# Small inputs in one transfer, six weight buffers for two sections, and the impulse response's matmuls placed behind named weight rows

## The chip, the cores and the metric

The kernel runs on one core of a Trainium2 chip. A core has a matrix engine (TensorE, PE in the profile; PEld is its weight load), three engines for elementwise work (VectorE or DVE, ScalarE or ACT, GpSimd or POOL) and a sync engine (SP) that issues most of the transfers. Every engine works through its own instruction list in order; engines wait for one another and for transfers through semaphores. The metric is the device time of one execution in microseconds (us). It was 2180.94 us in the median of three runs (2180.49 to 2183.13).

## The reference

One layer with two residual branches over x, of 4 batches x 1024 rows x 2048 columns, float32:

```
mod = silu(c) @ wmod                  # c: 4 x 2048, wmod: 2048 x (6*2048)
sa, ca, ga, sb, cb, gb = six sections of mod; ga, gb: sign kept, size at least 0.25
h = layernorm(x) * (1 + ca) + sa
x = x + ga * (causal convolution of each row of h with K, + D * h)
h = layernorm(x) * (1 + cb) + sb
x = x + gb * (h @ (W + low-rank updates).T + bias)
```

K, 2048 values, is the impulse response of a state space model with 64 complex states. It is computed from Lambda, p, q, Ct (64 complex numbers each), Vc (64 x 64 complex), Bp and log_step: a Cauchy sum at 2048 frequencies, a rational combination of four such sums, and an inverse Fourier transform.

## The kernel before

**Stages.** The kernel has a head, a first phase and a second phase. The first phase goes through 32 blocks of 128 rows: layer norm, modulation, transposition, the convolution as matmuls with a Toeplitz operand of K, gate and residual, second layer norm; the other four sections of `mod` and the merging of W with its low-rank updates are interleaved with it. The second phase multiplies 16 units of 256 rows with the merged weights (Winograd's form, seven products) in two halves.

**The head: two sections of mod.** A section is 16 *weight rows*. One weight row is a tile `wm` of 128 x 2048 float32 (1 MiB, loaded by `mod_load`, L309) and four matmuls by 128 columns x 512 (`mod_mm`, L314) that add into one PSUM tile `modps`. In this text r0 to r15 are the rows of section 1 (it gives `ca`), r16 to r31 those of section 0 (it gives `sa`), and r32 onward those of section 2. The pool of the `wm` tiles has three buffers (`WM = 3`), so the load of row n + 3 waits on SP until the four matmuls of row n are done. All rows and all blocks of x are issued on SP's queue, in order. After a section `mod_column` copies `modps` (ACT, `mrow`), transposes it (PE, `mtp`) and writes the column tile (DVE). `fold_scale` then finds a scale from `ca` and `sa` (a maximum over all partitions on POOL) and multiplies both. The first modulated activation (L535, `t<-tp,sa,ca`) needs that; it is where the convolution's operands begin.

**The head: the impulse response.** `toeplitz` calls `s4`. Sixteen transfers are issued on POOL's queue (L88 to L107): the vectors in two copies, `Vc` in two copies, `Bp`, `log_step`, and four tables. DVE computes scalars and numerators from them (L112 to L155). PE makes cosines and sines at 512 frequencies from the bfloat16 table `t_cs` (L161, `s4cs`), DVE and ACT make 1/w and the numerator from them (L165 to L173, a reciprocal among them), and PE sums over the states (L176, `s4rp`); this is done four times. Then come some forty small DVE instructions (L181 to L226), the transform (L229, `s4kp`), the scaling of K (L242 to L249, with a maximum on POOL), a store of K to DRAM (L254, `kd<-kk`), and a load of 128 shifted copies (L258, `kb<-kd`, 1 MiB). The last two are issued on ACT's queue. Four matmuls with a reversed identity follow (L262, `kbps`), and DVE makes the six fp16 operands `kh` and `kl` (L278 to L283).

**The order.** Most of it is a scheduler's, from the order in which the Python code emits work and from priorities. All of `toeplitz` up to the load of `kb` is emitted in one piece under `tc.high_priority()`, before any section. The part from L260 is emitted behind the matmuls of r22 (`KT = 6` in section 0) with `tc.issue_after`, which keeps later work from being placed ahead of that instruction. Blocks 0, 1 and 2 of x are loaded after r15.

**Completion lanes.** Transfers issued by SP and ACT share eight completion semaphores, handed out in turn. A transfer that gets a semaphore whose last transfer has not landed waits for that landing first, on the queue that issues it. In the kernel before, r23 waits in this way for the store `kd<-kk`, and r25 for the load `kb<-kd`.

The conditions of the head's loop and the constants that the change touches:

```
    for sec in (1, 0):
        for i, _ in enumerate(section(sec)):
            take(mer, M0)
            if sec == 0 and i == KT:
                with tc.issue_after(k.last.ins):
                    take(toe, 1)
        if sec == 1:
            for r in range(3):
                xs[r] = k.conv_load(pl, r)
```

Of the kernel before, what the change touches and what calls it, by code (L numbers as in the profile page):

```python
# [25 lines left out]
D = 2048          # length of a row: model width and sequence of the convolution  # L26
NB = 4            # batches
NC = D // P       # chunks of 128 in a row
HC = NC // 2
NU = 16           # units of 256 rows  # L30
LNMAX = 46.0      # no entry of a layer norm over 2048 exceeds sqrt(2047)
FP_TOP = 4096.0   # fp16 operands are scaled to at most twice this


class Net:
# [11 lines left out]
    # ---- scales: powers of two that bring the largest entry into [top, 2*top)  # L47
# [27 lines left out]
    # ---- impulse response of the state space model: PSUM [l1, l2], l = 16*l1 + l2  # L75
    def s4(self, pool):
# [7 lines left out]
        vec = T([P, 4, 2], "s4vec")  # L84
        vc = T([P, 64, 2], "s4vc")
        for h in range(2):
            hp = slice(64 * h, 64 * h + 64)
            nc.gpsimd.dma_start(out=vec[hp, 0, :], in_=io["Lambda_ri"])  # L88
            nc.gpsimd.dma_start(out=vec[hp, 1, :], in_=io["p_ri"])
            nc.gpsimd.dma_start(out=vec[hp, 2, :], in_=io["q_ri"])  # L90
            nc.gpsimd.dma_start(out=vec[hp, 3, :], in_=io["Ct_ri"].rearrange("o n c -> (o n) c"))
            nc.gpsimd.dma_start(out=vc[hp], in_=io["Vc_ri"])
        bp = T([P, 64], "s4bp")
        nc.gpsimd.dma_start(out=bp, in_=io["Bp"].rearrange("m o -> (m o)").partition_broadcast(P))
        ls = T([P, 1], "s4ls")
        nc.gpsimd.dma_start(out=ls, in_=io["log_step"].partition_broadcast(P))
        # cosines and sines in three bfloat16 parts, summed and broadcast by the tensor engine
        cs = T([3, 2, D], "s4cs", BF16)
        nc.gpsimd.dma_start(out=cs, in_=io["t_cs"])
        one = T([3, P], "s4one", BF16)  # L100
        v.memset(one, 1.0)
        csk = T([P, 2, 16], "s4csk")
        nc.gpsimd.dma_start(out=csk, in_=io["t_csk"])
        tw = T([P, 2, 16, 16], "s4tw")
        nc.gpsimd.dma_start(out=tw, in_=io["t_tw"])
        dft = T([P, 2, P], "s4dft")
        nc.gpsimd.dma_start(out=dft, in_=io["t_dft"])  # L107

        # 2/step = 2*exp(-log_step): range reduction, polynomial, exponent bits
# [16 lines left out]
        # B = Vc Bp  # L126
# [5 lines left out]
        # numerators conj(ct)B, conj(ct)p, conj(q)B, conj(q)p  # L132
# [15 lines left out]
        # 1/w, w = i (2/step) S - lambda C: real part in the first 64 rows, imaginary part below  # L148
# [8 lines left out]
        w = 512  # L157
        for c0 in range(0, D, w):
            cc, sc = (self.acc.tile([P, w], F32, tag="a", name="s4cs") for _ in range(2))
            for i, ps in enumerate((cc, sc)):  # L160
                nc.tensor.matmul(ps, one, cs[:, i, ds(c0, w)], start=True, stop=True)  # L161
# [11 lines left out]
            tt(nu, nu, wr, MUL)  # L173
            for c in range(w // P):
                g = c0 // P + c
                nc.tensor.matmul(  # L176
                    rp[:, g, :], nu[:, ds(P * c, P)], coef,
                    start=(g == 0), stop=(g == NC - 1), skip_group_check=True,
                )
# [36 lines left out]
        # inverse transform: over k2 with the table, over k1 on the tensor engine  # L216
# [5 lines left out]
        for o, (x, y, op) in enumerate(((ar, ai, SUB), (ai, ar, ADD))):  # L222
# [3 lines left out]
            v.tensor_reduce(zz[:, o, :], w1, AX.X, ADD)  # L226
        kp = self.tps.tile([P, 16], F32, tag="t", name="s4kp")
        for c in range(2):
            nc.tensor.matmul(kp, dft[:, c, :], zz[:, c, :], start=(c == 0), stop=(c == 1))  # L229
        return kp  # L230

    # ---- Toeplitz operand kb[s, j] = K[j - s], in two fp16 parts; D is added to K[0]
    def toeplitz(self, pool):
# [7 lines left out]
        kp = self.s4(pool)  # L241
        v.tensor_copy(kk, kp)  # L242
# [12 lines left out]
        # row s starts P - 1 - s earlier; the tensor engine puts the rows in the opposite order  # L255
# [8 lines left out]
        # for outputs in pairs of chunks: K at even chunks (for sums of two operands), and the  # L264
        # differences to the chunk before and after; two fp16 parts each
# [36 lines left out]
    # ---- one section of the modulation: PSUM rows 32 q + b hold columns 512 q ..  # L302
# [18 lines left out]
    def mod_column(self, pool, name, plus_one):  # L321
        """[d in chunk, chunk, batch] of the section in modps"""
# [12 lines left out]
    def mod_gate(self, pool, name, bias=None):  # L335
        """the gate by rows, in DRAM; with bias also gate*bias"""
# [23 lines left out]
    # ---- scales of the normalized, modulated rows, per batch; folded into the columns in place  # L360
# [15 lines left out]
    # ---- low-rank factors in two fp16 parts; w_e and the inverse scale of A go into B  # L376
    def prep_lora(self, pool, tmp):
# [9 lines left out]
        # no entry exceeds the norm of its row  # L387
# [32 lines left out]
    # ---- merged weights of d chunks c and c + 8; the seven right operands in DRAM  # L420
    def merge(self, pool, tmp, c):
# [22 lines left out]
        # no entry exceeds the norm of its row  # L444
# [44 lines left out]
    # ---- phase 1: layer norm, modulation, transposed operand of the convolution  # L489
# [29 lines left out]
    def conv_prep(self, pl, r, x, st, out):  # L519
# [4 lines left out]
        # fp16 parts of the chunks, and of the sums of an even chunk and the odd one after it  # L524
# [70 lines left out]
    def conv_late(self, x, y, sums):  # L595
        """gate and residual of a block whose convolution ran before the gate was there"""
# [6 lines left out]
    # ---- the second layer norm, transposed  # L603
# [21 lines left out]
    def gate_tile(self, pool, b):  # L625
        """the gate of a batch with the scales of the convolution's operands taken off, in all rows"""
# [14 lines left out]
    # ---- phase 2: left operands of the seven products of a unit  # L641
# [48 lines left out]
    def ffn_unit(self, pl, u, q, lf, wc):  # L690
# [34 lines left out]
        # Winograd's form; P4 comes with the opposite sign  # L725
# [28 lines left out]
M0, MR = 0, 2  # L754
# [3 lines left out]
WM = 3  # L758
LEFT0 = 30
KT = 6  # L760
# [11 lines left out]
def net(ctx: ExitStack, tc: tile.TileContext, io):  # L772
# [19 lines left out]
    def section(sec):  # L792
# [37 lines left out]
    toe = k.toeplitz(pool(st, "st", 1))  # L830
    with tc.high_priority():
        take(toe, 1)

    xs, hs = {}, {}
    sts = {}
    for sec in (1, 0):
        for i, _ in enumerate(section(sec)):
            take(mer, M0)
            if sec == 0 and i == KT:
                with tc.issue_after(k.last.ins):  # L840
                    take(toe, 1)
        if sec == 1:
            for r in range(3):
                xs[r] = k.conv_load(pl, r)
            for r in range(2):
                sts[r] = k.stats(pl, xs[r], "1")
    st.close()
    for name, bufs in (("h", 2), ("n", 2), ("t", 2), ("y", 2), ("g", 1), ("nt", 2)):
        pl[name] = pool(left, "p1" + name, bufs)
    def rest():  # L850
        mods = (x for sec in (4, 3, 5) for x in section(sec))
# [18 lines left out]
    def load_w(q, i):  # L870
        """the two halves of a right operand; two of them take the places of x"""
# [29 lines left out]
    sec = section(2)  # L901
# [80 lines left out]
def tables():  # L982
    """cosines and sines; they depend on the shapes alone"""
# [9 lines left out]
    csk = np.stack([np.cos(np.pi * kk / n), np.sin(np.pi * kk / n)], 1).astype(np.float32)  # L993
    ph = 2 * np.pi * (kk[:, None, :] * np.arange(16)[None, :, None] % n) / n
    tw = np.stack([np.cos(ph), np.sin(ph)], 1).astype(np.float32)
    a = 2 * np.pi * ((k1 * np.arange(P)[None]) % P) / P
    dft = (np.stack([np.cos(a), -np.sin(a)], 1) / n).astype(np.float32)
    return dict(t_cs=np.stack(parts), t_csk=csk, t_tw=tw, t_dft=dft)


def layout(inputs):
    g = {n.removeprefix("L0_attn_").removeprefix("L0_ffn_").removeprefix("L0_"): np.asarray(a) for n, a in inputs.items()}
    r = {n: g[n] for n in ("Lambda_ri", "p_ri", "q_ri", "Vc_ri", "Ct_ri", "Bp", "D", "log_step", "bias", "A", "coeffs", "scales", "c", "wmod")}
# [23 lines left out]
```

## Time and profile before

| | us |
|---|---|
| time, median of three runs (lowest to highest) | 2180.94 (2180.49 to 2183.13) |
| span of the profiled execution, first to last instruction | 2174.4 |
| median of the runs less that span | 6.5 |
| PE busy in the span | 2090.6 |
| first weight row's matmuls start | 6.51 |
| r31's matmuls start | 119.34 |
| first modulated activation starts | 125.73 |
| first matmul of the convolution starts | 128.88 |

The profiled execution's own device time is not listed beside its span; the median of the three runs stands in for it. A row of the table of waits reads: engine and line that waited, what it waited for, us in total, number of times, the longest. A row of the table by windows reads: the window, its length, busy us (and instructions) of PE, PEld, DVE, ACT and POOL, the granted PE clock as a share of full speed, the busy share of the 16 DMA engines, and GB/s. A timeline row reads: start, duration, engine, line, operation, tiles, shape, count, and in brackets the idle time before it and what ended it.

### The profile page before, as it was taken

How to read it: one execution, taken by the hardware profiler on the slowest of the kernel's cores; microseconds unless marked ns; L12 is line 12 of the kernel's file. 1: busy time of each engine (PE TensorE's matmuls, PEld its weight loads, DVE VectorE, ACT ScalarE, POOL GpSimd, SP SyncE). 2: the span in 40 equal slices, each digit the busy share in tenths (PEclk: the TensorE clock that was granted, in tenths of full speed). 3: DMA queues.
4: the chain of work that ended last, by engine and by line, in shares of the span. 5: the costliest groups of instructions: out<-in, count | busy, mean ns of one | idle time of the engine just before them, and what ended most of it. 6: DMA issues, size and time to landing. Idle time of an engine off the chain costs nothing.

```text
span 2174.4 us, 28541 instructions
## 1 busy us (share of the span) xinstructions
PE 2090.6 (96%) x11084; PEld 1020.7 (47%) x11084; DVE 1356.8 (62%) x2293; ACT 938.0 (43%) x1795; POOL 11.7 (1%) x28
## 2 busy tenths in 40 slices
PE   4699999999999999999999999999999999999998
PEld 1234555555555555565444444444444444444443
DVE  5637898888989999974666666666533333333333
ACT  0046877767867778863353545454300000000000
POOL 1000000000000000000000000000000000000000
PEclk6589999999999999999999999999999999999999
DMA  7988687888788656747766666666785544544541
GB/s 273 368 325 307 232 315 271 300 313 299 278 307 300 219 204 232 257 136 294 264 223 232 222 219 221 232 223 225 285 332 192 174 164 164 175 165 165 172 157 68
DMA packets 207307, 516.62 MB, mean 238 GB/s; under 512 B 16112, under 2 KB 81665, under 8 KB 180289
## 3 DMA queue, kind: packets, MB, share of 16 engines
q1 hardware_dynamic: 206208, 513.11, 66.3%
q8 instruction: 87, 1.43, 0.3%
q10 hardware_dynamic: 388, 1.16, 0.1%
q0 software_dynamic: 576, 0.54, 0.1%
q14 instruction: 48, 0.39, 0.1%
HBM read 325.89 MB, written 188.85 MB: 237 GB/s over the span
## 4 chain that ended last, share of the span: by engine, by line
PE 64%; DVE 13%; ACT 8%; DMA 6%; issue 2%; SPq 1%; DVEq 0%; ACTq 0%
PE fZ L701 18%; PE fY L701 12%; PE fX L701 11%; PE ya L564 9%; PE yb L564 5%; PE lps L440 3%; PE modps L314 3%; DMA gt<-n2d 2%; DVE lf L662 2%; ACT gt L651 2%; PE tp L620 2%; DVE s L668 1%; ACT t L535 1%; ACT n L611 1%; PE tp L532 1%
## 5 line engine op out<-in xcount | busy, mean ns | idle before, releaser
L701 PEld LDWEIGHTS <-lf 128*128 128x128 f16 x5376 | 526.4, 98 | 642.0 <-issue 10.2
L701 PE MATMUL fZ<-w,lf 128*128 128x512 f16 x2304 | 514.8, 380 | 6.2 <-ACT p L709 6.1
L701 PE MATMUL fX<-w,lf 128*128 128x512 f16 x1536 | 342.6, 379 | 0.0
L701 PE MATMUL fY<-w,lf 128*128 128x512 f16 x1536 | 342.5, 379 | 0.0
L564 PEld LDWEIGHTS <-hc 128*128 128x128 f16 x2304 | 215.7, 98 | 187.9 <-issue 31.9
L717 DVE TENSOR_TENSOR xo<-xo,gb 128x1024 f32<-128x1024 f32 x64 | 78.3, 1224 | 204.6 <-DMA xo<-x1d 204.5
L535 ACT ACTIVATE t<-tp,sa,ca 128x128 f32<-128x128 f32 x512 | 200.1, 471 | 6.0 <-DVE sa L373 3.8
L651 ACT ACTIVATE gt<-gt,sb,cb 128x256 f32<-128x256 f32 x256 | 132.1, 594 | 148.2 <-DMA gt<-n2d 147.4
L564 PE MATMUL ya<-kh,hs 128*128 128x512 f16 (+3 forms) x768 | 192.9, 326 | 0.9 <-ACT hs L543 0.9
L564 PE MATMUL ya<-kh,hc 128*128 128x512 f16 (+3 forms) x768 | 192.7, 326 | 0.5 <-ACT qs L577 0.5
L564 PE MATMUL yb<-kh,hc 128*128 128x512 f16 (+3 forms) x768 | 192.5, 326 | 0.0
L314 PE MATMUL modps<-wm,sct 128*32 128x512 f32 x768 | 132.1, 728 | 27.9 <-DMA wm<-in_wmod 27.9
L564 PEld LDWEIGHTS <-hs 128*128 128x128 f16 x1152 | 107.5, 98 | 96.9 <-issue 15.9
L709 ACT COPY p<-fZ 128x512 f32<-128x512 f32 x64 | 37.3, 583 | 256.9 <-PE fZ L701 256.9
L709 ACT COPY p<-fX 128x512 f32<-128x512 f32 x32 | 18.5, 578 | 268.7 <-PE fX L701 255.7
L564 PE MATMUL ya<-kl,hc 128*128 128x512 f16 (+3 forms) x384 | 125.1, 326 | 0.0
L564 PE MATMUL ya<-kl,hs 128*128 128x512 f16 (+3 forms) x384 | 125.1, 326 | 0.0
L564 PE MATMUL yb<-kl,hc 128*128 128x512 f16 (+3 forms) x384 | 125.1, 326 | 0.0
L661 ACT CAST lf<-s 128x1024 f16<-128x1024 f32 x64 | 67.2, 1050 | 102.5 <-DVE s L668 75.8
L621 ACT COPY nt<-tp 128x512 f32<-128x512 f32 x128 | 74.8, 597 | 60.0 <-PE tp L620 40.9
L544 DVE TENSOR_TENSOR hc<-t,hc 128x512 f16<-128x512 f32 x128 | 87.3, 682 | 6.3 <-ACT hc L543 5.8
L723 DVE TENSOR_TENSOR xo<-xo,fin 128x512 f32<-128x512 f32 x128 | 88.2, 689 | 3.1
(247 smaller groups left out, 2234.3 us busy)
## 6 DMA issues: line engine op xcount, KB each, us to landing
wm<-in_wmod SPq DMA_DIRECT2D x96, 1024.0 KB
lfd<-lf SPq DMA_DIRECT2D x112, 512.0 KB
lf<-lfd SPq DMA_DIRECT2D x112, 512.0 KB
x<-in_x SPq DMA_DIRECT2D x32, 1024.0 KB
x1d<-y SPq DMA_DIRECT2D x32, 1024.0 KB
n2d<-nt SPq DMA_DIRECT2D x128, 256.0 KB
gt<-n2d SPq DMA_DIRECT2D x128, 256.0 KB
xo<-x1d SPq DMA_DIRECT2D x64, 512.0 KB
```

Of the source, the lines that this page charges most:

```text
L314: self.last = self.nc.tensor.matmul(self.modps[32 * g : 32 * g + 32, :], self.sct[:, j].rearrange("p r b -> p (r b)"), w[:, ds(512 * g, 512)],
L440: nc.tensor.matmul(ps, la[:, x, k, h], y[:, k, osl], start=(n == 0), stop=(n == 5))
L535: nc.scalar.activation(t[:, k], tp[:, k], AF.Identity, bias=self.sa[:, c, b : b + 1], scale=self.ca[:, c, b : b + 1],)
L544: v.tensor_tensor(lo[:, sl], src, hi[:, sl], SUB)
L564: nc.tensor.matmul(pf[:, o:512], h, self.kf[f][z][:, ds(k0, 512 - o)], start=first, stop=(i == last and (x, z) == (1, 0)), skip_group_chec ...
L621: nc.scalar.copy(nt, tp)
L651: nc.scalar.activation(t[:, c], t[:, c], AF.Identity, bias=self.sb[:, c, b : b + 1], scale=self.cb[:, c, b : b + 1],)
L661: nc.scalar.copy(hl[:, :, 0, :], s)
L701: nc.tensor.matmul(ps[name], lf[i][:, k, x, :], wc[i][k // 4][:, k % 4, y, :], start=(first and n == 0), stop=(n == 3 * HC - 1), skip_grou ...
L709: nc.scalar.copy(t, ps[name])
L717: v.tensor_tensor(x, x, self.gbias, ADD)
L723: v.tensor_tensor(xs[r][:, h], xs[r][:, h], t, ADD)
```

## The change

There are three edits.

1. The small inputs and `c` are packed on the host's side of the layout into one array `small` of 128 x 265 float32, which SP loads first. The tables `csk`, `tw`, `dft` become one array `t_tab` of 128 x 800. `t_cs`, D and `t_tab` are loaded on ACT's queue. POOL issues no transfers any more.
2. Sections 1 and 0 take their weight rows in turn from two pools of three buffers (`wms` and `wm`), six in all. `wms` lies in the memory of the impulse response's own tiles, which is freed after section 0.
3. `s4` is a generator with stopping points. Its first part is emitted early as before. The parts that hold PE work are emitted behind weight rows counted by n over both sections (17 steps each): `KT = (0, 5, 8, 11, 14, 18, 27)`. The first two `s4cs` tables stand behind r0, the four `s4rp` sums behind r5 (in fact behind the first matmul of r6), r8, r11 and r14, the third and fourth table behind the second and third sum, the transform behind r17, and `kbps` behind r26. Blocks 0, 1, 2 of x are loaded after r20, r26 and r31; the statistics of blocks 0 and 1 follow their loads.

In the changed program's instruction lists DVE's 40 small instructions of `s4` come ahead of the three that make `sct` (the matmuls' left operand, which every weight row needs). The lanes fall differently: r3 waits for `t_cs`, r25 for the store `kd<-kk`, and the load of block 1 of x, with r27 to r31 behind it on SP, for the load `kb<-kd`. From some 1750 matmul instructions (of 19900 on PE) and some 120 transfers (of 900 on SP) onward, the lists of every engine are the same as before.

```
+        sm = self.small
+        vec = sm[:, 0:8].rearrange("p (i c) -> p i c", c=2)
+        vc = sm[:, 8:136].rearrange("p (n c) -> p n c", c=2)
+        bp, ls = sm[:, 136:200], sm[:, 200:201]
+
         cs = T([3, 2, D], "s4cs", BF16)
-        nc.gpsimd.dma_start(out=cs, in_=io["t_cs"])
+        nc.scalar.dma_start(out=cs, in_=io["t_cs"])
...
+        tab = T([P, 800], "s4tab")
+        nc.scalar.dma_start(out=tab, in_=io["t_tab"])
...
+        def table(c0):
+            cps[c0] = [self.acc.tile([P, w], F32, tag="a", name="s4cs") for _ in range(2)]
+            for i, ps in enumerate(cps[c0]):
+                nc.tensor.matmul(ps, one, cs[:, i, ds(c0, w)], start=True, stop=True)
+
+        yield
+        table(0)
+        table(w)
         for c0 in range(0, D, w):
-            cc, sc = (self.acc.tile([P, w], F32, tag="a", name="s4cs") for _ in range(2))
-            for i, ps in enumerate((cc, sc)):
-                nc.tensor.matmul(ps, one, cs[:, i, ds(c0, w)], start=True, stop=True)
+            if c0 >= 2 * w:
+                table(c0)
+            cc, sc = cps[c0]
...
             tt(nu, nu, wr, MUL)
+            yield
             for c in range(w // P):
...
+        yield
         kp = self.tps.tile([P, 16], F32, tag="t", name="s4kp")
...
-        c = pool.tile([P, NB, 16], F32, tag="mc", name="mc")
-        nc.sync.dma_start(out=c, in_=self.io["c"].rearrange("b (p j) -> p b j", j=16))
+        self.small = pool.tile([P, 265], F32, tag="small", name="small")
+        nc.sync.dma_start(out=self.small, in_=self.io["small"])
+        c = self.small[:, 201:265].rearrange("p (b j) -> p b j", j=16)
...
-WM = 3
+WM, WMS = 3, 3
+X0 = (21, 27)
 LEFT0 = 30
-KT = 6
+KT = (0, 5, 8, 11, 14, 18, 27)
...
-            k.mod_mm(k.mod_load(wmp, sec, q), q)
+            k.mod_mm(k.mod_load(pools[q % len(pools)], sec, q), q)
...
+    wms = pool(st, "wms", WMS)
     with tc.high_priority():
         take(toe, 1)
...
+    n = 0
     for sec in (1, 0):
-        for i, _ in enumerate(section(sec)):
-            take(mer, M0)
-            if sec == 0 and i == KT:
-                with tc.issue_after(k.last.ins):
+        for _ in section(sec, (wms, wmp)):
+            if n in KT:
+                with tc.issue_after(k.last.ins), tc.high_priority():
                     take(toe, 1)
-        if sec == 1:
-            for r in range(3):
+            if n in X0:
+                r = X0.index(n)
                 xs[r] = k.conv_load(pl, r)
-            for r in range(2):
                 sts[r] = k.stats(pl, xs[r], "1")
+            n += 1
+    xs[2] = k.conv_load(pl, 2)
     st.close()
```

More of the change, by code (lines that the diff above doesn't have):

```diff
@@ L82, in T @@
             return pool.tile(shape, dt, tag=name, name=name)
[L84 to L96, printed above, removed]
+        sm = self.small
+        vec = sm[:, 0:8].rearrange("p (i c) -> p i c", c=2)
+        vc = sm[:, 8:136].rearrange("p (n c) -> p n c", c=2)
+        bp, ls = sm[:, 136:200], sm[:, 200:201]
         cs = T([3, 2, D], "s4cs", BF16)
-        nc.gpsimd.dma_start(out=cs, in_=io["t_cs"])
+        nc.scalar.dma_start(out=cs, in_=io["t_cs"])
         one = T([3, P], "s4one", BF16)
         v.memset(one, 1.0)
[L102 to L107, printed above, removed]
+        tab = T([P, 800], "s4tab")
+        nc.scalar.dma_start(out=tab, in_=io["t_tab"])
+        csk = tab[:, 0:32].rearrange("p (c k) -> p c k", c=2)
+        tw = tab[:, 32:544].rearrange("p (c k n) -> p c k n", c=2, k=16)
+        dft = tab[:, 544:800].rearrange("p (c k) -> p c k", c=2)
         z = T([P, 4], "s4z")
@@ L157, in s4 @@
         w = 512
+        cps = {}
+        def table(c0):
[5 more added lines that the diff above has]
+        table(w)
         for c0 in range(0, D, w):
-            cc, sc = (self.acc.tile([P, w], F32, tag="a", name="s4cs") for _ in range(2))
-            for i, ps in enumerate((cc, sc)):
-                nc.tensor.matmul(ps, one, cs[:, i, ds(c0, w)], start=True, stop=True)
+            if c0 >= 2 * w:
+                table(c0)
+            cc, sc = cps[c0]
             wi = pool.tile([P, w], F32, tag="s4wi", name="s4wi", bufs=2)
@@ L229, in s4 @@
             nc.tensor.matmul(kp, dft[:, c, :], zz[:, c, :], start=(c == 0), stop=(c == 1))
-        return kp
+        self.kp = kp
     def toeplitz(self, pool):
@@ L240, in toeplitz @@
         kk = pool.tile([P, 16], F32, tag="kk", name="kk")
-        kp = self.s4(pool)
-        v.tensor_copy(kk, kp)
+        yield from self.s4(pool)
+        v.tensor_copy(kk, self.kp)
         dt = pool.tile([1, 1], F32, tag="dt", name="dt")
@@ L752 @@
 ACTNORM = ""
-M0, MR = 0, 2
+MR = 2
 ACC, TPS = 5, 2
@@ L790, in net, with section @@
     k.prep_mod(msm)
-    def section(sec):
+    def section(sec, pools):
         for q in range(16):
@@ L850, in rest @@
     def rest():
-        mods = (x for sec in (4, 3, 5) for x in section(sec))
+        mods = (x for sec in (4, 3, 5) for x in section(sec, (wmp,)))
         n = 0
@@ L899, in stats @@
         sts[r] = k.stats(pl, xs[r], "1")
-    sec = section(2)
+    sec = section(2, (wmp,))
     take(prep(0), 9)
@@ L992, in tables @@
     kk = k1 + P * np.arange(16)[None]
-    csk = np.stack([np.cos(np.pi * kk / n), np.sin(np.pi * kk / n)], 1).astype(np.float32)
+    csk = np.stack([np.cos(np.pi * kk / n), np.sin(np.pi * kk / n)], 1)
     ph = 2 * np.pi * (kk[:, None, :] * np.arange(16)[None, :, None] % n) / n
-    tw = np.stack([np.cos(ph), np.sin(ph)], 1).astype(np.float32)
+    tw = np.stack([np.cos(ph), np.sin(ph)], 1)
     a = 2 * np.pi * ((k1 * np.arange(P)[None]) % P) / P
-    dft = (np.stack([np.cos(a), -np.sin(a)], 1) / n).astype(np.float32)
-    return dict(t_cs=np.stack(parts), t_csk=csk, t_tw=tw, t_dft=dft)
+    dft = np.stack([np.cos(a), -np.sin(a)], 1) / n
+    tab = np.concatenate([t.reshape(P, -1) for t in (csk, tw, dft)], 1).astype(np.float32)
+    return dict(t_cs=np.stack(parts), t_tab=tab)
 def layout(inputs):
     g = {n.removeprefix("L0_attn_").removeprefix("L0_ffn_").removeprefix("L0_"): np.asarray(a) for n, a in inputs.items()}
-    r = {n: g[n] for n in ("Lambda_ri", "p_ri", "q_ri", "Vc_ri", "Ct_ri", "Bp", "D", "log_step", "bias", "A", "coeffs", "scales", "c", "wmod")}
+    r = {n: g[n] for n in ("D", "bias", "A", "coeffs", "scales", "wmod")}
+    half = [g[n].reshape(64, -1) for n in ("Lambda_ri", "p_ri", "q_ri", "Ct_ri", "Vc_ri")]
+    both = np.tile(np.concatenate(half, 1), (2, 1))
+    rows = [np.broadcast_to(g[n].reshape(1, -1), (P, g[n].size)) for n in ("Bp", "log_step")]
+    r["small"] = np.concatenate([both, *rows, g["c"].reshape(NB, P, 16).transpose(1, 0, 2).reshape(P, -1)], 1)
     r["x"] = g["u"].reshape(-1, D)
```

## The prediction

> **What bounds the kernel now.** I read PE's waits before and after 130 us first, then SP's waits in the head, then the head cut into windows, then the timeline where the head ends.
>
> PE's waits, and SP's, from 0 to 130 us:
>
> ```profile
> PE modps L314 <- DMA wm<-in_wmod: 27.9, 18, 6.5
> PE s4cs L161 <- DMA s4cs<-in_t_cs: 9.4, 1, 9.4
> PE s4rp L176 <- DVE s4nu L173: 6.0, 4, 2.2
> ...
> SPq L309 <- PE modps L314: 81.4, 32, 14.9
> SPq L309 <- DMA wm<-in_wmod: 23.5, 13, 5.7
> SPq L309 <- DMA kb<-kd: 5.7, 1, 5.7
> ```
>
> PE waits for weight rows, and SP, which loads them, waits for PE to free a buffer. PE works in order, so a matmul of the impulse response that stands in line (9.4 us for `t_cs`) also holds up the weight rows behind it, and with three buffers the loads then stop. The windows show it:
>
> ```profile
> 30.00:34.00 4.00, 2.38 (x6) 0.59 (x4) 3.72 (x16) 0.00 (x0) 0.00 (x0) 0.50 0.03 9
> ...
> 77.00:82.00 5.00, 3.88 (x20) 0.40 (x16) 3.99 (x17) 0.20 (x1) 0.00 (x0) 0.51 1.01 415
> ...
> 93.00:100.00 7.00, 6.88 (x12) 2.68 (x16) 1.19 (x3) 1.17 (x2) 0.00 (x0) 0.58 0.61 243
> ...
> 129.00:160.00 31.00, 30.97 (x193) 12.18 (x191) 12.72 (x25) 16.38 (x43) 0.00 (x0) 1.00 0.86 309
> 160.00:200.00 40.00, 40.00 (x249) 19.90 (x246) 26.24 (x50) 19.47 (x40) 0.00 (x0) 1.00 0.85 310
> ```
>
> Where nothing stops it the DMA runs at a share of 1.01 and 415 GB/s, or 2.5 us for each 1 MiB row (r17 to r20 start at 75.16, 77.65, 80.15 and 82.68). From 30 to 34 us it stands still, and from 93 to 105 it is two thirds busy. From 129 us PE is full. So the program is a head bound by transfers with holes, then a long stretch bound by PE: over 129 to 700 us PE is busy 562 of 571 us. What the head saves, the end should save.
>
> The tail of the head, on the timeline:
>
> ```profile
> 70.88 0.17 DVE L242 COPY kk<-s4kp 128x16 f32<-128x16 f32 x1 [0.53 <-PE s4kp L229]
> ...
> 77.99 0.35 ACTq L254 DMA_DIRECT2D kd<-kk  x1
> ...
> 82.95 0.35 ACTq L258 DMA_DIRECT2D kb<-kd  x1
> ...
> 93.12 6.57 PE L262 MATMUL kbps<-kb,rev 128*128 128x512 f32 x8 [1.25 <-DMA kb<-kd]
> ...
> 119.34 1.93 PE L314 MATMUL modps<-wm,sct 128*32 128x512 f32 x8 [0.56 <-DMA wm<-in_wmod]
> ...
> 125.73 1.51 ACT L535 ACTIVATE t<-tp,sa,ca 128x128 f32<-128x128 f32 x4 [3.75 <-DVE sa L373]
> ```
>
> K's operands are ready at 108.5 (last L283), 13 us before the rows; the last row's matmuls end at 121.3, and 4.4 us later modulation starts. I forecast that start.
>
> **Edit 1, the inputs.** Sixteen transfers leave POOL's queue (some 0.55 us of issue each, up to 25.2 us); one enters SP's ahead of r0 (0.46, in place of `mc`'s) and two ACT's ahead of the table load (0.35 to 0.53 each). `small`: the nearest row is `mc`, issued at 0.72 and landed by 2.85, so 2.1 us; the upper bound is `t_cs` on POOL's queue, 8.0. I take 2.1, since it is the same queue at the same empty time. DVE's 40 small instructions took 0.54 + 1.08 + 4.37 = 6.0 us in their three groups, so they run from 2.9 to 8.9; `sct` follows with 1.1 (3.14 to 4.23) at 10.0, against 4.2 before. Every weight row is behind it: r0 starts on PE at 10.0, not 6.51. Six buffers cover this: r5 would land at 6.5 + 5 x 2.5 = 19. With three buffers it would cost up to 3.5 us. `t_cs` lands between 2.9 and 8.7, before PE asks at 11.9 and before r3, which waits for it, is needed on the wire (12). `t_tab` has until about 51. All of that costs nothing.
>
> **Edit 3, the chain of the impulse response.** On PE: r0 10.0 to 11.9; four `s4cs` of 0.43, to 13.6. On DVE from 12.8: two tables side by side, each 4 x 0.67 + 0.6 + 3.3 + 0.6 = 7.2, so 14.4, to 27.2; the first `s4rp` can start at 26.6. PE has been standing inside r6 since 22.5; it does the sum (1.0), three quarters of r6 (1.45), r7 and r8 (1.94 each), the second sum and the third table (1.9): 34.8. DVE idles from 27.2 to 34.3, then works 7.2: 41.5. Sum, table, DVE again: 42.9 to 50.1; last sum to 51. L181 to L226 took 63.01 to 70.23, so 58.2. PE meanwhile does r15, `mrow`, `mtp`, r16, r17 (1.94 + 0.7 + 1.1 + 3.9): 58.6. Transform 0.6: `kk` at 59.4, against 70.88. From `kk` to the store 7.1 us passed before, with 4.9 us of statistics of x between; these now stand behind, so 2.2: 61.6. Store 4.96, issue 0.35, load of `kb` 9.8 (83.3 to 93.1, on a full DMA): **kb lands at T = 77**, against 93.1. Bounds: the store between 2.1 (`mc`) and 10 (twice its row), the load between 5.2 (r0, issued 1.24, landed 6.48) and 15 (six rows of 2.5 ahead of it). I keep the rows of the same two transfers.
>
> Here the granted clock enters. My rows of 1.94 are at 0.50; at full clock one takes 1.06 (r23 to r25, at 1.00). Rows at 2.5 us leave PE 78% busy at 0.51 in the window above, so I keep 1.94. The Trainium skill ("TensorE: Matmul & The Clock Gate", Part 1: The HAM clock gate) says that some 3.4 us of sustained work release full clock; then the rows that PE does back to back behind a sum would be quicker, and by an estimate from that page T would be 4 us earlier.
>
> **Edit 2, six buffers.** A row's load need not wait while PE is less than about 10.5 us behind (five rows of 2.5, less 2 of issue ahead). By the chain above PE is 11.7 behind at r16, the worst: at most 1.2 us is lost, against some 24 us before (r31 reached PE 112.8 us after r0, for 36 MiB at 2.5, or 89). What stops next is SP: r25 waits for the store (66.6, about when its buffer comes free), and block 1 of x for T, with r27 to r31 behind it. On an idle wire a transfer takes 5.2: x1 lands at T + 5.2, r31 at T + 17.7. The rows give `sa` at + 3.84 (119.34 to 123.18): T + 21.5. DVE gives it no earlier: `kbps` from about T + 1 with 6.57, the last copy at T + 9, then 13.0 of DVE work (L278 to L283 8.8 before, two L511 of 1.3, half the statistics of block 1): T + 22.4, just later. From `sa` to modulation 2.55 before, plus three of block 2's statistics at 0.67 that now stand between: T + 27, or 26.5 by overlap.
>
> **The sum.** 77 + 26.5 = 103.5, against 125.73: 22.2 us earlier. Behind it the lists are reordered only to about 250 us, with no work added; I put that at 0, within 3 either way (PE idles 4.4 us in 200 to 240). 2174.4 - 22.2 = 2152.2, plus the 6.5 between span and median: **2159 us**.
>
> The wire's floor: behind r0 come 31 rows, two blocks, `kb` and 0.5 MiB of small inputs, so r31 starts at 6.5 + 34.5 x 2.5 = 92.8 at the earliest; modulation follows 6.4 later (119.34 to 125.73 before) plus two statistics of 0.67, at 100.6: no more than 25 us to gain. A rule speaks against this. The Trainium skill ("DMA: Bandwidth & Descriptors", Where 436 GB/s comes from) lets the HBM side bind such loads at about 358 GB/s. By an estimate from it the rows take 2.9 us, r31 lands near 108 and the gain is about 10. The rows above at 411 to 428 GB/s decide for 2.5.
>
> **The rivals.**
> - *The wire alone* (T at 72 or less): the chain of sums is overstated, as before it took 38.6 us from first table to `kk` and I have 46.6. Gain 25, 2156.
> - *The two small transfers of K are slower behind six queued rows*: store and load at 10 and 15, T = 87, modulation at 113.5, gain 12, 2169. For: they share the engines with a fuller queue. Against: the queue was never empty in 77 to 93 either (1.01).
> - *SP's stop becomes the bound, and it is slower*: x1 and five rows queue behind `kb`. At T = 99.2 modulation is where it was; each us beyond is lost. At T = 106, 2188. That needs 29 us more than my chain: several PE stops at the sums growing together. Against: DVE's work starts 19 us earlier (32.3 to 12.8).
> - *No effect*: later transfers hold the end. Against: PE's share over 129 to 700.
>
> **How the numbers follow.** Forecast 0.57, its own range 2156 to 2164; wire alone 0.16; slower K transfers 0.14; slower 0.09; none 0.04. Below 2153 the wire's floor and the 3 us leave little. The range 2153 to 2173 leaves out the two last cases and some of the third. The runs differ by 0.12%, so 0.2% (4.4 us) is about what can be told. Faster 0.86, same 0.05, slower 0.09.
>
> **What would show it.** First modulated activation at 101 to 107; r0 on PE near 10; `kb` landed by 80; DMA share near 1.0 from 5 to 65 us; a hole after `kb`; PE's waits after the head as before. I am wrong if `kb` lands beyond 95, if PE waits for weight rows in section 2, or if the granted clock after the head is below 1.00.

## The result, and the profile after

The changed kernel takes 2166.0 us in the median (2165.34 to 2167.89, four runs), the kernel before beside it 2182.0 (2180.49 to 2184.97): a ratio of 0.9932, with a 95% interval of 0.9918 to 0.9946. It is 16 us (0.7%) faster; 22 were forecast. The spans of the two profiled executions are 2174.4 and 2163.6 us, only 10.8 apart.

The waits of the changed kernel, 0 to 115 us, as engine, line and what was waited for; then us in total, number, longest:

```profile
PE modps L317 <- DMA wm<-in_wmod: 21.0, 12, 6.7
DVE s4wi L165 <- PE s4cs L153: 14.1, 3, 8.2
...
PE s4rp L177 <- DVE s4nu L173: 9.8, 3, 5.7
PE modps L317 <- DVE sct L300: 9.1, 1, 9.1
...
SPq L312 <- PE modps L317: 58.0, 24, 9.3
SPq L312 <- DMA wm<-in_wmod: 20.1, 8, 4.7
SPq L312 <- DMA kd<-kk: 8.2, 1, 8.2
SPq L519 <- DMA kb<-kd: 7.1, 1, 7.1
```

The 9.4 us that PE stood for `t_cs` are gone. New are DVE's wait of 8.2 us for the third table, which PE makes only behind the second sum, and SP's two waits in a row for K's store and load. The windows of the same kernel (length, busy us of PE, PEld, DVE, ACT, POOL, the granted clock, DMA share, GB/s):

```profile
7.00:20.00 13.00, 9.03 (x44) 1.69 (x44) 9.75 (x22) 2.30 (x4) 0.54 (x2) 1.00 1.02 424
20.00:40.00 20.00, 14.36 (x74) 4.85 (x74) 11.04 (x10) 1.21 (x2) 0.00 (x0) 0.74 1.01 417
...
72.00:77.00 5.00, 1.74 (x12) 0.16 (x8) 0.55 (x3) 1.49 (x2) 0.00 (x0) 0.69 0.45 125
...
112.00:160.00 48.00, 48.00 (x312) 20.60 (x311) 18.77 (x39) 25.73 (x66) 0.00 (x0) 0.97 0.88 307
```

The wire (the 16 DMA engines) is full from 7 to 60 us and nearly so to 68; the one large hole that is left is SP's stop at 72 to 77. PE is full from 112 us, where before it was from 129. The tail of the head, on the timeline:

```profile
34.56 0.75 DVE L165 TENSOR_SCALAR s4wi<-s4cs,s4ts 128x512 f32<-128x512 f32 x1 [8.17 <-PE s4cs L153]
...
56.03 0.37 DVE L182 COPY s4R<-s4rp 128x128 f32<-128x128 f32 x1 [1.97 <-PE s4rp L177]
...
64.07 0.17 DVE L244 COPY kk<-s4kp 128x16 f32<-128x16 f32 x1 [1.41 <-PE s4kp L231]
66.24 0.36 ACTq L256 DMA_DIRECT2D kd<-kk  x1
73.69 0.36 ACTq L260 DMA_DIRECT2D kb<-kd  x1
81.71 0.33 SPq L519 DMA_DIRECT2D x<-in_x  x1
...
86.09 4.39 PE L264 MATMUL kbps<-kb,rev 128*128 128x512 f32 x8
...
100.07 1.58 PE L317 MATMUL modps<-wm,sct 128*32 128x512 f32 x8 [0.69 <-DMA wm<-in_wmod]
...
107.03 1.85 ACT L538 ACTIVATE t<-tp,sa,ca 128x128 f32<-128x128 f32 x5 [4.65 <-DVE sa L376]
```

Modulation starts at 107.03, 18.7 us earlier than before. So by these two profiles 8 of the 18.7 are lost again behind the head. To find where, I matched DVE's and ACT's instructions of two profiles by line and order, and took the median difference of their starts in stretches of the time of before; below this is called the *lead* over the profile before. It is 17.0 us at 160 to 170, 14.7 at 220 to 230, 9.1 at 260 to 280, 9.7 at 500 to 600 and 10.7 at the end. The loss lies between 180 and 260 us. ACT's timeline of the changed kernel there, and the windows beside it:

```profile
216.61 3.90 ACT L417 ACTIVATE lb<-lb,lsb_s 128x2048 f32<-128x2048 f32 x2
220.41 3.68 ACT L418 CAST lbh<-lb 128x2048 f16<-128x2048 f32 x2
224.00 0.61 ACT L546 CAST hc<-t 128x512 f16<-128x512 f32 x1
```

```profile
200.00:210.00 10.00, 7.82 (x55) 5.08 (x56) 9.55 (x26) 10.00 (x26) 0.00 (x0) 1.00 0.85 287
210.00:220.00 10.00, 4.62 (x33) 2.10 (x34) 9.75 (x26) 9.77 (x19) 0.54 (x1) 0.86 0.97 357
220.00:230.00 10.00, 9.47 (x46) 3.69 (x39) 8.72 (x17) 9.32 (x18) 0.00 (x0) 0.80 0.83 310
```

In one block of 7.4 us ACT does the last work on the two low-rank factors (scaling, fp16 copy); the next cast of the modulation stands behind it, at 224.00. PE is busy 21.9 of these 30 us, and the granted clock falls to 0.80. The kernel before does the same four instructions apart, with modulation between them, and PE is busy 26.1 of its 30 us:

```profile
225.89 1.99 ACT L414 ACTIVATE lb<-lb,lsb_s 128x2048 f32<-128x2048 f32 x1
228.83 1.89 ACT L415 CAST lbh<-lb 128x2048 f16<-128x2048 f32 x1
232.00 2.02 ACT L414 ACTIVATE lb<-lb,lsb_s 128x2048 f32<-128x2048 f32 x1
234.71 1.92 ACT L415 CAST lbh<-lb 128x2048 f16<-128x2048 f32 x1
```

```profile
210.00:220.00 10.00, 8.44 (x57) 4.30 (x55) 9.94 (x24) 10.00 (x27) 0.00 (x0) 1.00 0.87 307
220.00:230.00 10.00, 7.68 (x49) 4.49 (x45) 9.97 (x30) 9.87 (x18) 0.40 (x1) 0.93 0.91 331
230.00:240.00 10.00, 10.00 (x49) 4.75 (x49) 8.57 (x13) 10.00 (x19) 0.00 (x0) 0.90 0.72 248
```

But the block is not what PE waits for most. PE's timeline of the changed kernel shows where it stands:

```profile
214.21 0.66 PE L535 MATMUL tp<-ident,n 128*128 128x128 f32 x4 [1.11 <-ACT t L538]
216.77 0.72 PE L535 MATMUL tp<-ident,n 128*128 128x128 f32 x4 [1.90 <-ACT t L538]
219.14 1.93 PE L317 MATMUL modps<-wm,sct 128*32 128x512 f32 x8 [1.65 <-DMA wm<-in_wmod]
...
223.46 0.61 PE L443 MATMUL lps<-lbh,lac 128*128 128x512 f16 x1
```

Of the 8 us that PE idles from 200 to 222, 5.8 lie ahead of the block's start at 216.61, at transposes that wait for ACT's copies and activations while ACT is busy throughout (10.00 and 9.77 of 10 us). During the block PE stands 2.3 us, nearly all of it, by the profile, for weight rows. So the block marks the place where the order is bad; that it is itself the cause is not shown.

No edit touches this work. The scheduler orders the lists anew when the head changes, and this came out of it.

### The profile page after: what moved, and what is told of

Read it like the earlier page. It is cut to its first block, busy times and chain, and to the rows that moved or that the text cites. A ratio compares the mean times of both kernels' runs of the same rounds, so it can differ in the third digit from the quotient of the medians.

```text
span 2163.6 us, 28506 instructions
## 1 busy us (share of the span) xinstructions
PE 2080.5 (96%) x11084; PEld 1019.0 (47%) x11084; DVE 1355.8 (63%) x2293; ACT 938.8 (43%) x1795; POOL 2.8 (0%) x12
## 4 chain that ended last, share of the span: by engine, by line
PE 63%; DVE 15%; DMA 10%; ACT 9%; issue 2%; SPq 1%; POOL 0%; DVEq 0%; ACTq 0%
PE fZ L704 19%; PE fY L704 12%; PE fX L704 11%; PE ya L567 8%; PE yb L567 4%; PE modps L317 3%; DMA gt<-n2d 3%; PE lps L443 2%; ACT gt L654 2%; DVE lf L665 2%; PE tp L623 2%; ACT t L538 2%; ACT n L614 2%; DMA wm<-in_wmod 1%; DMA xo<-x1d 1%
## 5 line engine op out<-in xcount | busy, mean ns | idle before, releaser
L538 ACT ACTIVATE t<-tp,sa,ca 128x128 f32<-128x128 f32 x512 | 199.6, 466 | 10.2 <-DVE sa L376 4.7
L317 PE MATMUL modps<-wm,sct 128*32 128x512 f32 x768 | 123.5, 687 | 32.2 <-DMA wm<-in_wmod 23.1
L567 PEld LDWEIGHTS <-hs 128*128 128x128 f16 x1152 | 107.6, 98 | 98.0 <-issue 17.7
L535 PE MATMUL tp<-ident,n 128*128 128x128 f32 x512 | 79.4, 279 | 13.1 <-ACT t L538 11.6
```

Of the source, the lines that this page charges most:

```text
L317: self.last = self.nc.tensor.matmul(self.modps[32 * g : 32 * g + 32, :], self.sct[:, j].rearrange("p r b -> p (r b)"), w[:, ds(512 * g, 512)],
L535: nc.tensor.transpose(tp[:, k], n[:, ds(P * (c0 + k), P)], self.ident)
L538: nc.scalar.activation(t[:, k], tp[:, k], AF.Identity, bias=self.sa[:, c, b : b + 1], scale=self.ca[:, c, b : b + 1],)
L567: nc.tensor.matmul(pf[:, o:512], h, self.kf[f][z][:, ds(k0, 512 - o)], start=first, stop=(i == last and (x, z) == (1, 0)), skip_group_chec ...
```

## The experiments

Theory A: the head's gain is that of the early inputs and the six buffers, bounded by the chain of the impulse response up to `kb`. Theory B: the block on ACT gives back 7 to 8 us. Rivals: one edit alone is the whole gain; the placement (edit 3) is what it is worth; SP's stop is the bound; a lead is given back later whatever is done.

All results together. "Mod" is the first modulated activation in the kernel's profile; the lead is in us, as defined above, at 160 to 170, 260 to 280, 500 to 600 and the end; the ratio goes to the runs of the kernel before on the same chip.

| kernel | r31 on PE | mod | lead | median us (range) | ratio (95%) |
|---|---|---|---|---|---|
| before | 119.34 | 125.73 | | 2182.0 (2180.5 to 2185.0) | |
| after | 100.07 | 107.03 | 17.0, 9.1, 9.7, 10.7 | 2166.0 (2165.3 to 2167.9) | 0.9932 (0.9918 to 0.9946) |
| e1_buffers | 108.69 | 114.43 | 9.9, 9.9, 7.1, 5.5 | 2170.7 (2169.9 to 2174.0) | 0.9954 (0.9936 to 0.9971) |
| e2_inputs | 111.46 | 117.86 | 7.9, 6.0, 2.7, 1.7 | 2170.1 (2168.6 to 2174.4) | 0.9948 (0.9929 to 0.9967) |
| e3_three | 107.64 | 115.40 | 9.9, 0.4, 1.5, -3.1 | 2177.9 (2174.3 to 2180.6) | 0.9981 (0.9970 to 0.9992) |
| e4_lora | 101.90 | 108.32 | 18.6, 19.0, 16.1, 4.5 | 2173.7 (2164.8 to 2178.8) | 0.9961 (0.9945 to 0.9978) |
| e5_onepiece | 97.40 | 105.16 | 20.1, 13.0, 14.3, 14.3 | 2163.5 (2161.3 to 2165.3) | 0.9917 (0.9903 to 0.9931) |
| e6_pool | 95.16 | 103.77 | 21.5, 13.3, 12.9, 6.1 | 2165.1 (2163.5 to 2170.0) | 0.9927 (0.9913 to 0.9942) |
| e7_tables | 95.06 | 103.82 | 21.7, 14.8, 15.2, 11.1 | 2163.1 (2161.0 to 2164.9) | 0.9913 (0.9898 to 0.9927) |
| e8_best | 93.09 | 100.87 | 24.5, 25.4, 22.9, 5.1 | 2166.3 (2162.7 to 2170.9) | 0.9931 (0.9915 to 0.9946) |
| e9_lora2 | 99.10 | 107.22 | 18.1, 15.3, 17.1, 18.1 | 2162.6 (2157.9 to 2167.2) | 0.9929 (0.9914 to 0.9943) |
| e10_best2 | 97.03 | 103.46 | 21.8, 17.2, 19.9, 16.8 | 2160.0 (2156.8 to 2166.0) | 0.9917 (0.9901 to 0.9933) |
| e11_after_again | 99.39 | 107.13 | 18.2, 9.3, 10.5, 9.4 | 2165.1 (2163.0 to 2166.6) | 0.9935 (0.9922 to 0.9948) |
| e12_before_again | 119.70 | 126.10 | -0.4, -0.4, -0.6, -1.3 | 2181.2 (2177.0 to 2185.0) | 0.9994 (0.9979 to 1.0009) |

Single profiles scatter. Four with the changed kernel's head (after, e4, e9, e11) have modulation at 107.0 to 108.3; e7 and e8, whose heads are the same code, at 103.8 and 100.9 (the clock granted from 40 to 60 us was 0.50 in e7, and 0.67 and 0.70 in e8's two windows there). So a difference of some 3 us between two heads is not told by one profile each.

### Each of the first two edits alone

**e1_buffers**, six buffers in the kernel before:

```
-            k.mod_mm(k.mod_load(wmp, sec, q), q)
+            k.mod_mm(k.mod_load(pools[q % len(pools)], sec, q), q)
...
+    wms = pool(st, "wms", 3)
```

> The kernel before with edit 2 alone: six weight buffers, inputs and impulse response as before. My theory (the impulse response sets the pace, the buffers only let the rows follow): K still reaches the operand load near 83 us, kb lands near 93, r25 and the rows behind it wait for it on SP, r31 starts on PE near 112 and the first modulated activation near 118, against 125.73 before and 107.03 after; 2174 to 2176 us. Rival (the buffers are the change): r31 near 100, modulation at 110 or earlier, 2168 or less. Rival (the buffers do nothing without the early inputs): modulation at 124 to 126, 2181.

Modulation came at 114.43: better than my theory by 3.6 us, short of the rival by 4.4. `kk` was 1.6 us earlier than before (69.26), `kbps` 5.1 us (88.06, not 93.12): the store's step took 3.3 us instead of 4.96. The time, 2170.7, lies below the theory's 2174 to 2176 too.

**e2_inputs**, the packed inputs in the kernel before: `small` on SP's queue, `t_cs` and `t_tab` on ACT's, three buffers, the impulse response in one piece.

> The kernel before with edit 1 alone: packed inputs on SP's and ACT's queues, three buffers, impulse response in one piece ahead of the rows. My theory: DVE begins the tables near 13 us and kb lands near 70, but PE stands in line for DVE until about 40 with three rows loaded, so the wire stops for some 15 us; the rows become the bound, r31 starts near 108 and modulation near 115; 2171 us. Rival (early inputs are the whole gain): modulation at 108 or earlier, 2166. Rival (rows stop as long as before): modulation at 123 to 126, 2180.

`kk` was ready at 46.09, and still modulation began at 117.86, since the rows were late: theory right in kind, 2.9 us off. Each edit alone gives part of the gain at modulation, 11.3 and 7.9 us. In time each alone gives 10 to 11 us by its ratio, two thirds to three quarters of the whole: both keep before's order of ACT's four instructions and lose 0 and 1.9 us of lead there (160 to 280 us), where the changed kernel loses 7.9.

### Without edit 2, and without edit 3

**e3_three**, the changed kernel with three buffers:

```
-    wms = pool(st, "wms", WMS)
...
-        for _ in section(sec, (wms, wmp)):
+        for _ in section(sec, (wmp,)):
```

> The changed kernel without edit 2: three weight buffers. My theory: in the changed kernel the wire stood at 125 GB/s from 72 to 77 us, since SP waited for K's store and load; that slack takes most of what three buffers lose in front of it (some 2 us at r0 and 3 at each of three sums), and what is left delays the sums, so modulation starts at 109 to 113 against 107.03; 2168 to 2172. Rival (the buffers are the change): modulation at 116 or later, 2175 or more. Rival (buffers worth nothing): 107, 2166.

A miss: modulation at 115.40 lies between theory and rival, the time (2177.9) with the rival. The slack at SP's stop did not absorb the loss, since the wire was slower all the way (windows of this kernel):

```profile
10.00:30.00 20.00, 15.58 (x66) 4.06 (x65) 14.26 (x14) 2.30 (x4) 0.54 (x2) 0.73 0.92 340
...
50.00:70.00 20.00, 15.22 (x68) 4.82 (x71) 11.25 (x51) 0.58 (x1) 0.41 (x1) 0.50 0.91 338
```

340 GB/s against 417 with six buffers; block 0 of x was issued at 63.11 instead of 51.01, and SP never caught up. Six buffers are worth 8.4 us at modulation on top of the other two edits, and some 11 us of time by the two ratios.

**e5_onepiece**, the changed kernel with the impulse response ahead of the rows as before:

```
-KT = (0, 5, 8, 11, 14, 18, 27)
+KT = (27,)
...
-        take(toe, 1)
+        take(toe, 7)
```

> The changed kernel without edit 3: the impulse response emitted in one piece ahead of the rows, as in the kernel before; only the four matmuls of K's operand (kbps) stay behind r26. My theory: DVE has no 8 us wait for the third table, so the scaled K is ready some 10 us earlier (the copy kk near 53 instead of 64.07) and kb lands near 71; PE stands in line for DVE until about 40 and the six buffers cover all but 5 to 8 us of that, so r31 and modulation come out within 4 us of 107: 103 to 111, 2163 to 2170. Rival (the placement is what the change is worth): modulation at 114 or later, 2174 or more.

As the theory had it, and lower still for `kk`. Timeline of this kernel:

```profile
45.46 0.17 DVE L244 COPY kk<-s4kp 128x16 f32<-128x16 f32 x1 [0.70 <-PE s4kp L231]
...
54.25 0.37 ACTq L260 DMA_DIRECT2D kb<-kd  x1
...
83.93 3.70 PE L264 MATMUL kbps<-kb,rev 128*128 128x512 f32 x8
...
97.40 1.94 PE L317 MATMUL modps<-wm,sct 128*32 128x512 f32 x8 [1.44 <-DMA wm<-in_wmod]
...
105.16 1.85 ACT L538 ACTIVATE t<-tp,sa,ca 128x128 f32<-128x128 f32 x5 [5.12 <-DVE sa L376]
```

`kk` is 18.6 us earlier than in the changed kernel, because DVE never waits for a table, and modulation is 1.9 earlier. The edit that places the impulse response behind chosen rows brings nothing once the six buffers are there: they cover PE's stand at the tables. By medians the kernel without it is 2.5 us quicker, with overlapping intervals. With three buffers it may help the head: modulation at 115.40 in e3, 117.86 in e2, 2.5 us apart, which is within the scatter of single heads. (That e3 is still the slower of these two, 2177.9 against 2170.1, goes with its lead, which falls from 9.9 to 0.4 around the block on ACT, while e2 keeps before's order there.) That the 18.6 us bring so little has its reason in the rows: r31 waits for its transfer (1.44), and `kbps`, left behind r26, waits for its turn.

### SP's stop, and the tables

**e6_pool**, K's store and load on POOL's queue (`nc.gpsimd.dma_start` for `kd` and `kb`):

> The changed kernel with K's store and load issued on POOL's queue, whose completion semaphores SP does not share, so that r25 and block 1 of x no longer wait for them. My theory: the 15 us of SP's waiting cost little, since DVE's work behind kb (the operands of K, statistics) ends together with the rows: modulation at 105.5 to 108, 2164 to 2167, while r31 starts 4 to 8 us earlier than 100.07. Rival (SP's stop is the bound): modulation at 99 to 103, 2158 to 2162. Rival (kb on a full wire lands later): kb at 85 or later, modulation at 109 to 111, 2168 to 2170.

Between theory and rival. SP's waits are gone (waits of this kernel), r31 starts 4.9 us earlier and modulation 3.3:

```profile
SPq L312 <- PE modps L317: 67.6, 29, 7.9
SPq L312 <- DMA wm<-in_wmod: 23.4, 11, 7.1
...
```

So the stop costs up to 3 us at modulation, no more (the scatter of single heads is as large), and the median, 2165.1, shows no gain. What binds behind it is DVE, as the prediction had it: `kb` lands no earlier (81.57, where `kbps` starts at once), the last of K's operands is ready at 97.11 (100.19 in the changed kernel), and with the two L514 that follow DVE comes to `sa` at 99.87, 0.9 us after PE's `mtp`.

**e7_tables**, third and fourth pair of tables behind r4, the four sums behind r14, the transform behind r18 (`KT = (0, 4, 14, 19, 26)`):

> The changed kernel with the third and fourth pair of cosine and sine tables behind r4 instead of behind the second and third sum, all four sums behind r14 and the transform behind r18: DVE then has all its work without a wait. My theory (the chain through DVE sets T, and T sets modulation until the wire does): kk near 53 against 64.07, kb landed near 71 against 81.7, modulation at 100 to 103 against 107.03; about 5 us less at the end, 2160 to 2162, if the lists behind the head stay as they are. Rival (the rows bind): kb early, r31 still near 100 and modulation at 106 to 107, 2165 to 2166.

`kk` came at 61.60, not 53: DVE was done with the tables near 40 and then stood, because PE reached the sums behind r14 at 45.13 and took 7.0 us for the four, at a granted clock of 0.50. The longest wait of DVE in this kernel, and PE's sums:

```profile
DVE s4R L187 <- PE s4rp L182: 12.2, 1, 12.2
```

```profile
45.13 7.00 PE L182 MATMUL s4rp<-s4coef,s4nu 128*128 128x8 f32 x32
```

I moved the wait from the tables to the sum. Modulation at 103.82 is 3.2 us earlier with a `kk` only 2.5 us earlier, about as much as heads scatter; this run doesn't separate the theory from its rival.

### The block on ACT

**e4_lora**, the last loop of `prep_lora` in steps:

```
         for k in range(2):
+            yield
             nc.scalar.activation(b[:, k], b[:, k], AF.Copy, scale=sb)
             nc.scalar.copy(self.bh[:, k], b[:, k])
...
-        k.prep_lora(pl["lora"], pl["mrg"])
+        yield from k.prep_lora(pl["lora"], pl["mrg"])
```

> The changed kernel with the four last activations of the low-rank factors (two scalings and two fp16 copies of 128x2048) emitted one factor at a time, so that ACT has them apart as in the kernel before, not in one block of 7.6 us. The head is unchanged: modulation at 107.0. My theory: that block, at 216 to 224 us in the changed kernel, held up the transposes that feed PE, and gave back about 7 of the 17 us won by then; spread, the lead over the kernel before stays at 15 to 17 us beyond 250 us and the time is 2158 to 2161. Rival (the lead was lost to something else, and the block only stands near it): no change, 2165 to 2167.

At the place itself the loss is gone: the lead is 17.8 us before the block's place (180 to 200) and 19.0 behind it. The time is a miss: 2173.7. Between 500 and 1400 us the lead falls to 5. The two new steps moved every later step of the merging by two, and the lists of the engines then differ from the changed kernel's up to about 1000 us, longer than I wrote beforehand for the run after it. PE's waits from 500 to 900 us, first of the changed kernel, then of this one:

```profile
PE tp L535 <- ACT t L538: 3.5, 5, 1.0
```

```profile
PE tp L536 <- ACT t L539: 10.2, 7, 2.8
```

**e8_best**, e4 and e7 together:

> The changed kernel with the early tables and with the low-rank factors' activations apart: both causes together. If each theory holds, modulation at 100 to 103 and no loss between 180 and 250 us: 2152 to 2156. If only the tables count: 2160 to 2162. If only the low-rank block counts: 2158 to 2161. If neither: 2165 to 2167.

Modulation at 100.87, the lead 25.4 us behind the block's place and still 22.9 at 500 to 600, and then the same fall as in e4, to 5.1; the time, 2166.3, is that of "neither". As e4, it left open whether the moved steps or the lead itself was the cause.

**e9_lora2** tells these apart: it spreads the block as e4 does, and leaves the later steps in place.

```
-        for _ in mer:
-            yield
-            n += 1
-            if n % MR == 0:
+        for i, _ in enumerate(mer):
+            if i != 2 and i != 3:
+                yield
+            n += i > 1
+            if i > 1 and n % MR == 0:
```

> As the earlier run with the low-rank factors' activations apart, but with the later steps of the merging left where they are in the changed kernel: the two steps added there moved everything that is interleaved behind them, and the lists of the engines differed for some 500 us; here they are the changed kernel's again from PE's 1380th row of its list, at some 300 us. Modulation at 107. My theory (the block of 7.6 us on ACT gives back 7 us; what the earlier run lost between 500 and 1000 us came from the moved steps): the lead over the profile before stays at 16 to 20 us from 250 to 1000 us, and the time is 2157 to 2161. Rival (a lead is given back later whatever the block does): 2164 to 2168.

The lead is 18.1 before the block, 15.3 behind it, 17.1 at 500 to 600 and 18.1 at the end: in the end nothing is given back. The moved steps are told by the times as well: e4 and e9 differ in them alone, and their ratios are 0.9961 and 0.9929 with intervals that do not overlap. (One profile does not exclude a later loss: e9's is its quickest execution, and in e6's, its slowest, the lead falls from 12.9 to 6.1 behind 500 us with no step moved.) ACT's timeline and the windows of this kernel:

```profile
216.60 2.00 ACT L418 ACTIVATE lb<-lb,lsb_s 128x2048 f32<-128x2048 f32 x1
219.31 1.90 ACT L419 CAST lbh<-lb 128x2048 f16<-128x2048 f32 x1
224.25 2.04 ACT L418 ACTIVATE lb<-lb,lsb_s 128x2048 f32<-128x2048 f32 x1
226.62 1.95 ACT L419 CAST lbh<-lb 128x2048 f16<-128x2048 f32 x1
```

```profile
200.00:210.00 10.00, 9.87 (x69) 6.09 (x67) 9.86 (x24) 10.00 (x23) 0.00 (x0) 1.00 0.88 290
210.00:220.00 10.00, 7.83 (x48) 3.03 (x48) 9.79 (x26) 9.98 (x24) 0.67 (x1) 1.00 1.00 378
220.00:230.00 10.00, 8.81 (x52) 4.76 (x49) 7.29 (x11) 9.16 (x14) 0.00 (x0) 1.00 0.82 281
```

The same head, the same four instructions, and PE is busy 26.5 of 30 us at full clock, against 21.9 at a clock down to 0.80. All profiles say the same: the six of the changed kernel's order (after, e3, e5, e6, e7, e11) lose 7 to 10 us of lead between 160 and 280 us, the six with the four instructions apart (e1, e2, e4, e8, e9, e10) between nothing and 5. So in the traces this order loses 8.1 us at this place on average, the others 1.3. That the block on ACT is what costs it is not shown. In the 18 us ahead of the first of the four instructions PE idles 5.4 to 6.2 us in the six, 0.1 to 2.3 in the others and in the kernel before; from the first to the last it idles 1.8 to 2.9 us in the six and 0.6 to 2.7 in the others. And the split moved more than ACT's list: in the changed kernel 24 matmuls of the convolution (`ya<-kh,hs`, `ya<-kl,hs`) run from 223.9 us, behind the `lps` that needs the block's cast; in e9 they run between 202.6 and 211.1, where the changed kernel's PE stands (e4 has 45 more ahead of the block). That fits the idle time better than the block does, but no run moves the one without the other. In the times less is seen: e9 is 2.5 us below e11 on the same chip, over a range of 2157.9 to 2167.2, and their ratios, 0.9929 and 0.9935, are not told apart.

**e11_after_again**, the changed kernel beside e9 and e10:

> The changed kernel once more, beside the two others on the same chip: modulation at 106 to 108.5, the block of the low-rank activations at 216 to 224 us, 2164 to 2168 by either theory. It gives the step that those two are measured against.

As expected: 107.13 and 2165.1; its profile loses the lead at the same place (18.2 to 9.3).

**e10_best2**, e5 with e9, and `kbps` behind r22 (`KT = (23,)`):

> The changed kernel without edit 3 (impulse response in one piece ahead of the rows), with the matmuls of K's operand behind r22 in place of r26, and with the low-rank activations apart and the later steps left in place. My theory: kb lands near 62, DVE has the operands of K before the rows end, r31 starts near 95 and modulation near 101 to 103; with no loss at the block the time is 2152 to 2157. Rival (a lead is given back later): 2162 to 2166.

`kbps` starts at 73.97, ten us before e5's, and r31 stays at 97.03: the head is now bound by the rows. Modulation is 6.4 us behind r31, as in the kernel before. With 2160.0 it has the lowest median of all, 5.1 us below e11 on the same chip, though short of the 2152 to 2157 expected and with intervals that overlap; its ratio, 0.9917, is that of e5, which keeps the block together.

### The base

**e12_before_again**, the kernel before once more:

> The kernel before once more, for a second profile: its first profile has a span of 2174.4 us, which is about 2176 with what lies around a span, while the median of its runs is 2180 to 2182. If the first profile caught an execution that was quick behind the head, the second has the same head (modulation at 125 to 126.5, PE idle for the same stretches) and loses its 3 to 6 us beyond 250 us; then the lead of the changed kernel at its end is larger than the two first profiles show by as much. If it is the head that varies, modulation starts at 128 or later.

The head is the same (126.10), and so is nearly all the rest: the profiled execution took 2177.6 us, again one of the quicker ones. Where executions of 2182 us and more of the kernel before lose their time no profile shows; that stays open.

## Why the prediction was right, and where it missed

The sign, the mechanism in the head and the range 2153 to 2173 held; 2166.0 lies 2 us above the forecast's own range, 2156 to 2164. The gain at modulation was 18.7 us of 22.2 forecast, and 8 of it were lost behind the head. By the prediction's steps:

- **The inputs.** `small` landed by 3.72, not 2.85, DVE's small work took 4.2 us instead of 6.0, and r0 started at 9.09, forecast 10.0. Nothing was lost by it: the wire was full from 7 us.
- **The chain of the impulse response** is the term that was too small, by 4.7 us: `kk` at 64.07, forecast 59.4. The third table stood where I had it (DVE's work on it starts at 34.56, forecast 34.3). A single table then took DVE 8.3 us, twice, not 7.2: 0.76 of that is DVE's stand for ACT's square, the rest is spread over the passes. Sum and table took 2.9 between the two, not 1.4, and the last sum 2.0, not 0.9: the prediction priced a sum at 1.0, near the 1.06 of the first one before, while the other three before took 1.87 to 1.88, and so did three of the four here. How much of the 3.5 us at modulation this cost is not shown: in e5 `kk` is 18.6 us earlier and modulation 1.9.
- **Six buffers** were to cut the wire's loss from some 24 us to 1.2. The wire was full from 7 to 60 us (1.00 to 1.02). They cover more than I drew from that: e5 shows that with them the chain can stand in line ahead of the rows. I costed edit 3 as the step that lets PE and DVE work side by side; it also made DVE wait 14.1 us for tables, and it brings nothing.
- **From `kk` to `kb`**: 2.2 to the store as forecast. The store's step took 7.45 and not 4.96, the load with its issue 8.0 and not 10.2; the sum, 15.5, was right (15.1) by luck, with both parts wrong. `kb` landed at 81.7, forecast 77, nearly all of it the chain's error.
- **From `kb` to modulation**: 25.3, forecast 26.5. r31 came T + 18.4 (17.7), `sa` T + 21.4 (22.4). That SP's stop and DVE's work end together was right; taking the stop away (e6) gave 3.3 us.
- **The wire's floor** of 100.6 for modulation: the best head, e8's, reached 100.87.
- **The clock.** I kept 1.94 for a row. PE worked without a break from the first sum at 25.86; its rows still took 1.94 and that sum 1.88, the second sum, at 32.94, took 1.06, and the three rows behind it 2.78 together. The rule of the Trainium skill ("TensorE: Matmul & The Clock Gate", Part 1: The HAM clock gate), that some 3.4 us of sustained work release full clock, fits in kind; here it took about 7, and the rows between the first two sums, for which the chain waited, stayed slow. T came later, not 4 us earlier. The rule of "DMA: Bandwidth & Descriptors" (Where 436 GB/s comes from) that the HBM side binds at about 358 GB/s is contradicted by 417 to 424 GB/s over 13 to 20 us here.
- **"Behind it the lists are reordered ... I put that at 0, within 3 either way"**: this step failed. It cost 7.9 us of lead between 160 and 280 us, where the lists differ: PE idles and its clock falls around the block on ACT. The lists were at hand, and both the four instructions of 2 us that had come together and the convolution's matmuls behind them could be seen there; I looked for added work, and there was none. Which of the two it is stays open, and the times of e9 and e11 don't confirm the size.
- **The base.** I added to the span the 6.5 us by which it lay below the median. What lies around a span is 1.7 us in the changed kernel and 2.0 in the kernel before; the rest was the profiled execution of before being quick. That error hid part of the other two: 22.2 less 3.5 (head) less 7.9 (behind the head) is the 10.8 between the profiles, and 5.2 more between the medians makes 16.0.

Of the rivals, the slower store and load had the right time for the changed kernel (2169 against 2166) with a mechanism that did not happen: T moved, by the chain.

## What to carry to other kernels

A change that lets a scheduler order its lists anew is costed over the whole stretch in which they differ: look for long instructions of a second engine that have come together, and for ready work of the bound engine that has moved behind something that waits, for each us that PE idles there is lost where PE is otherwise full. Then see where the bound engine's idle time lies: here most of it lay ahead of the block that caught the eye. A gain at one place is followed along the timeline until it is at the end, by the difference of starts of the same instructions, and an experiment that adds a step to an interleaved sequence must leave the steps behind it in place, or it measures those. Where more buffers cover a stop, the reordering that was to avoid the stop may be worth nothing; make the variant without it.

## What was not expected of the hardware

An 8 KB store among these loads is slow and uneven: from issue to the instruction that waits for it 4.96 us in the kernel before, 3.3 in e1, 6.6 in e5 and e6, 7.5 in the changed kernel and in e7. In the changed kernel PE was busy 4.62 of the 10 us from 210 to 220, and the granted clock was 0.86 there and 0.80 in the next 10 us; in e9, with 7.83 of 10, it stayed at 1.00. That makes idle time dearer: from 200 to 230 PE idled 8.1 us against e9's 3.5, and the lower clock took up to 3.4 more (0.14 x 10 + 0.20 x 10), by this estimate up to 8.0 us in all. The sums of e7 ran at 0.50 from 45 to 52 us although PE was busy 8.9 and 9.2 of 10 us around them.
